# Linear attention's quotient written as a mean less a small term, with a new table of ranks

## The chip, the core and the metric

The kernel runs on one core of a Trainium2 chip. A core has a matrix engine (TensorE, PE in the profile; its weight loads are listed apart as PEld), a vector engine (DVE), a scalar engine for activations (ACT), a general engine (POOL) and a queue that starts transfers (SP). The metric is the device time of one execution in microseconds, the median of several runs.

## The reference, cut to what matters

The whole is two transformer layers on x of 8 x 512 x 128: linear attention, an fp4 feed-forward, causal softmax attention, and a mixture of experts, each behind a layer norm and added to x. The change lies in the first of these:

```python
q = jnp.einsum('bsi,ihd->bshd', x, wq) + bq
k = jnp.einsum('bsi,ihd->bshd', x, wk) + bk
v = jnp.einsum('bsi,ihd->bshd', x, wv) + bv
Q = _feature_map(q)          # elu(t) + 1
K = _feature_map(k)
KV = jnp.einsum('bshd,bshd->bhd', K, v, precision=HI)
Ksum = jnp.sum(K, axis=1)
Z = 1.0 / (Q * Ksum[:, None, :, :] + EPS)       # EPS = 1e-06
attn = Q * KV[:, None, :, :] * Z
out = jnp.einsum('bshd,hdo->bso', attn, wo) + bo
return jax.nn.gelu(out)
```

There are 8 batches (b), 512 positions (s), 16 heads of 64 (h, d): 1024 features. For one feature and one batch, KV and Ksum are single numbers, and the quotient is Q·KV / (Q·Ksum + EPS), position by position.

## The kernel before

The kernel does not issue instructions directly. Its calls are recorded as steps (class `Plan`), each with a rank, and `Plan.ordered` then puts them into one order for all engines, with a model of each step's length: whenever an engine is free, it takes the ready step of the lowest rank whose buffers are to be had. All recorded instructions are issued from one line, 407, so the profile tells them apart by the names of their tiles. `HURRY` and `EMPTY` lower the rank of a dense matmul after an idle stretch, and of the step that reads a PSUM buffer last. `kept_warm` puts matmuls on zeros (tile `mid<-zeros,ident`) into gaps of TensorE's order. Steps on `nc.either` may go to DVE or POOL.

The work of one batch is cut into stages, or lanes: loads, norm, linear, out, fp4, attention, routing, experts. Each call of a stage takes the next entry of the table `TURNS`; `Span` gives the stage's steps ranks that rise along it. In the program the linear attention and fp4 stages of batch b come with the softmax attention, routing and experts of batch b - 1; the ranks decide how they are mixed. PSUM has two double buffers (`pair`), one for the attention outputs (`mid`) and three single ones (`ahead`); a half of a `pair` may be lent to `ahead`.

Linear attention works with features on the 128 partitions and positions along the row, in 8 tiles (c) of 128 features for each batch. For a tile, `elu` multiplies xnT by the weights, and makes elu (less one or not) of it with two ACT steps and one DVE step. `features(c)` does it for k, whose sum over positions comes out of the same DVE step (ks), sums the product with v (kv), does q, and prepares:

- `qf`, q's feature plus one (ACT, `qf<-qf,one_sb`), and `z` = qf·ks + 1e-6 (ACT, `z<-qf,eps_sb,s`);
- `kb` = ks·bv + kv on DVE in one-column steps (`s<-s` and `s<-s,bqkv_sb,s`), and `wk_o`, the output weights with their rows scaled by kb (ACT).

`products(c)` joins two tiles so that one reciprocal does for both: r = z0·z1, q0·z1 and q1·z0 (three products, `r<-z,z` and `qf<-qf,z`), then 1/r on DVE in two halves, then two products with r (`qf<-qf,r`). All of these products stand on POOL. `linear_out` sums the eight matmuls of `wk_o` with these tiles in two groups of four, adds bo, and goes on with the gelu.

On sizes: xnT has two buffers, qf seven, z three, wk_o five; the one-column sums come from twelve buffers `s1`.

Of the kernel before, what the change touches and what calls it, by code (L numbers as in the profile page):

```python
# [9 lines left out]
F32 = mybir.dt.float32  # L10
# [3 lines left out]
AF = mybir.ActivationFunctionType  # L14
ALU = mybir.AluOpType
AX = mybir.AxisListType

P = 128
# [20 lines left out]
class View:  # L39


    def __init__(self, buf, shape, path=()):
        self.buf, self.shape, self.path = buf, tuple(shape), path
# [91 lines left out]
class Plan:  # L135
# [45 lines left out]
    def one_go(self):  # L181
        return OneGo(self)
# [1 line left out]
    def together(self):  # L184
        return Together(self)

    def span(self, lane, low, high):
        return Span(self, lane, low, high)

    def add(self, engine, method, a, k):  # L190
        step = self.open
# [57 lines left out]
    def ordered(self):  # L249
# [12 lines left out]
            for b in s.uses:  # L262
                users[b] = len(b.users)
        ready_at = {s: 0.0 for s in self.steps}
        empties = set()
        for s in self.steps:
            for b in s.uses:
                if b.tag in self.psum and s.engine != "tensor" and (False or max(b.users, key=lambda u: u.number) is s):
                    empties.add(s)
        waiting = {e: [] for e in self.engines}  # L270
        for s in self.steps:
            if not left[s]:
# [11 lines left out]
        while done < len(self.steps):  # L284
            for e in self.HOP:
                while busy[e] <= now:
# [3 lines left out]
                    ahead = HURRY if e == "tensor" and clock.idle(now) else 0.0  # L290
                    for s in sorted(
                        ready,
                        key=lambda s: (s.rank - (ahead if s.work > 0.6 * s.cost else 0.0) - (EMPTY if s in empties else 0.0), s.number),
                    ):
                        if s.port and port > now:
                            continue
                        asked = {}
                        for b in s.takes:
                            asked.setdefault(b.tag, []).append(b)
                        if not all(  # L300
                            all(b in turns[s.lane, t][-len(bs) :] for b in bs)
                            for t, bs in asked.items()
                        ):
                            continue
                        if all(
                            (t not in kept or stuck) and free.has(t, len(bs)) for t, bs in asked.items()
                        ):
                            best = s
                            break

                        kept.update(asked)
# [197 lines left out]
class Span:  # L509


    def __init__(self, plan, lane, low, high):
        self.plan, self.lane, self.low, self.high = plan, lane, low, high

    def __enter__(self):
        self.plan.lane = self.lane
# [2 lines left out]
    def __exit__(self, *_):  # L519
        steps = self.plan.steps[self.first :]  # L520
        total, done = sum(s.cost for s in steps) or 1.0, 0.0
        for s in steps:
            s.rank = self.low + (self.high - self.low) * done / total
            done += s.cost


# [86 lines left out]
def cost(engine, method, out, ins, a, k):  # L613
# [32 lines left out]
    if engine == "gpsimd":  # L646
# [17 lines left out]
    *((f"s4 {lane}", [P, NT], 10, F32) for lane in LANES),  # L664
    ("s1", [P, 1], 12, F32),
    ("xn", [P, NT, D], 1, F32),
    ("xnT", [P, S], 2, F32),
    ("kf", [P, S], 2, F32),
    ("qf", [P, S], 7, F32),
    ("z", [P, S], 3, F32),  # L670
    ("r", [P, S], 1, F32),
    ("y", [P, S], 2, F32),
    ("wk_o", [P, D], 5, F32),
    ("xf", [P, NT, D], 2, F32),
    ("xfT", [P, S], 1, F32),
    ("sc", [P, 44], 4, F32),
# [26 lines left out]

TURNS = {
    "loads": (
        (-3.318, -1.909), (-0.316, -0.059), (0.897, 0.897), (1.614, 1.925),
        (2.836, 3.009), (4.433, 4.682), (4.978, 4.978),
    ),  # L710
    "norm": (
        (-2.124, -2.124), (-0.875, -0.875), (0.083, 0.200), (1.422, 1.904),
        (2.231, 2.231), (3.002, 3.606), (3.880, 4.108), (5.162, 5.409),
    ),
    "linear": (
        (-1.500, -0.940), (-0.500, 0.050), (0.419, 0.790), (2.088, 2.088),
        (2.612, 3.162), (3.422, 3.979), (4.158, 4.730), (4.805, 5.222),
    ),
    "out": (
        (-1.176, -0.826), (-0.386, -0.123), (0.618, 0.709), (1.508, 1.508),  # L720
        (2.508, 3.214), (3.335, 3.734), (4.601, 4.985), (5.739, 6.093),
    ),
    "fp4": (
        (-1.986, -1.736), (-0.900, -0.500), (0.154, 0.510), (1.010, 1.218),
        (2.103, 2.516), (3.487, 3.887), (3.993, 4.270), (5.177, 5.177),
        (5.602, 6.278),
    ),
    "attention": (
        (-0.500, 0.000), (0.000, 0.909), (0.934, 1.761), (2.198, 3.044),
        (3.241, 3.877), (3.954, 4.849), (5.114, 5.848), (6.017, 7.017),  # L730
        (7.193, 8.226),
    ),
    "routing": (
        (1.913, 2.213), (2.979, 3.308), (4.000, 4.223), (5.196, 5.230),
        (6.538, 6.538), (7.103, 7.746), (8.148, 8.148), (8.956, 9.346),
    ),
    "experts": (
        (2.400, 2.713), (3.217, 3.986), (4.222, 5.211), (5.438, 6.138),
        (6.531, 6.863), (7.391, 8.138), (8.571, 9.439), (9.499, 10.378),
    ),  # L740
}

# [2 lines left out]
def block_kernel(  # L745
# [138 lines left out]
    neghalf = const.tile([P, NT], F32, name="neghalf", tag="neghalf")  # L884
    dev.gpsimd.memset(neghalf, -0.5)

    rank = const.tile([P, NT, E], F32, name="rank", tag="rank")
    for e in range(E):
        dev.gpsimd.memset(rank[:, :, e : e + 1], float(E - e))
    eps_sb = const.tile([P, 1], F32, name="eps_sb", tag="eps_sb")  # L890
    dev.gpsimd.memset(eps_sb, 1e-6)
    one_sb = const.tile([P, 1], F32, name="one_sb", tag="one_sb")
    dev.gpsimd.memset(one_sb, 1.0)

    vas = [const.tile([P, NT, H1, VW], F32, name=f"va{i}", tag=f"va{i}") for i in range(2)]
    for t in vas:
# [81 lines left out]
    def linear_attention(b):  # L978

        xnT = normed.pop(b)  # L980

        def elu(c, i, w, tag, **accum):

            pw = new("ahead", [P, S])
            nc.tensor.matmul(pw, w[c // 2][:, ts(c % 2, P)], xnT, start=True, stop=True)
            f = new(tag, [P, S])
            bias = bqkv_sb[:, i, c : c + 1]
            nc.scalar.activation(f, pw, AF.Relu, bias=bias)
            nc.scalar.activation(pw, pw, AF.Exp, bias=bias)
            nc.vector.scalar_tensor_tensor(f, pw, -1.0, f, ALU.add, ALU.min, **accum)  # L990
            return f

        def features(c):

            ks, kv, kb = (new("s1", [P, 1]) for _ in range(3))
            kf = elu(c, 1, wqkv[1], "kf", accum_out=ks)
            nc.vector.tensor_scalar(ks, ks, float(S), None, ALU.add)
            pw = new("ahead", [P, S])
            nc.tensor.matmul(
                pw, wqkv[2][c // 2][:, ts(c % 2, P)], xnT, start=True, stop=True  # L1000
            )
            nc.vector.scalar_tensor_tensor(pw, kf, 1.0, pw, ALU.add, ALU.mult, accum_out=kv)

            nc.vector.tensor_scalar(
                kb, ks, bqkv_sb[:, 2, c : c + 1], kv, ALU.mult, ALU.add
            )
            qf = elu(c, 0, wqkv[0], "qf")
            nc.scalar.activation(qf, qf, AF.Identity, bias=one_sb)
            z = new("z", [P, S])
            nc.scalar.activation(z, qf, AF.Identity, bias=eps_sb, scale=ks)  # L1010
            wk_o = new("wk_o", [P, D])
            nc.scalar.activation(wk_o, wo_sb[c // 2][:, c % 2, :], AF.Copy, scale=kb)
            return qf, z, wk_o

        def products(c):


            (q0, z0, w0), (q1, z1, w1) = features(c), features(c + 1)
            r = new("r", [P, S])
            nc.either.tensor_tensor(r, z0, z1, ALU.mult)  # L1020
            nc.either.tensor_tensor(q0, q0, z1, ALU.mult)
            nc.either.tensor_tensor(q1, q1, z0, ALU.mult)
            for part in (slice(0, 256), slice(256, S)):
                nc.vector.reciprocal(r[:, part], r[:, part])
            nc.either.tensor_tensor(q0, q0, r, ALU.mult)
            nc.either.tensor_tensor(q1, q1, r, ALU.mult)
            return [(w0, q0), (w1, q1)]

        return [p for c in range(0, NC0, 2) for p in products(c)]

    def linear_out(b, pairs):
        y = new("y", [P, S])
        for half in range(2):
            po = new("ahead", [P, S])
            with together():
                for i, (wk_o, qz) in enumerate(pairs[4 * half : 4 * half + 4]):
                    nc.tensor.matmul(po, wk_o, qz, start=(i == 0), stop=(i == 3))
            if half == 0:
                nc.scalar.activation(y, po, AF.Identity, bias=bo_sb)
            else:  # L1040
                nc.vector.tensor_tensor(y, po, y, ALU.add)

        g = new("y", [P, S])
        nc.scalar.activation(g, y, AF.Square)
# [447 lines left out]
    def stage(lane, what, *args):  # L1492
        with plan.span(lane, *next(turns[lane])):
            return what(*args)

    for b in range(NB):
        if b > 1:
            xs[b] = stage("loads", load_x, b)
        normed[b] = stage("norm", normed_T, xs[b], "ahead", "xn", "xnT")
        pairs = stage("linear", linear_attention, b)  # L1500
        stage("out", linear_out, b, pairs)
        if b == 0:
            stage("fp4", fp4_weights)
        stage("fp4", fp4_feed_forward, b)
# [77 lines left out]
```

## Time and profile before

| | us |
|---|---|
| median of three runs | 1132.38 (1130.52 to 1133.14) |
| the profiled execution | 1131.95 |
| its span, first to last instruction | 1130.1 |
| first exponential of the softmax attention starts | 198 |
| last attention output normalised | 1054 |

The profiled execution is 1.85 us longer than its span; all times in the profile count from the span's start. Busy shares are means over the span. The granted clock of TensorE was 0.982 of full speed on average; it was below 1.0 in most slices of the first 226 us. A float32 matmul of 128x128 weights shows up as two records. A row of groups gives the line, the engine, the operation, the tiles written and read, the sizes and count; behind the bar, the busy time, the mean of one in ns, and the engine's idle time just before it with what ended most of it.

### The profile page before, as it was taken

The page shows a single profiled execution, that of the slowest core. Times are in us where ns is not written, and L with a number is a line of the kernel's source. Part 1 is how long each engine was busy: PE and PEld are TensorE (multiplying, and loading weights), DVE is VectorE, ACT ScalarE, POOL GpSimd, SP SyncE. Part 2 cuts the span into 40 slices and gives each one's busy share as a digit, 9 for nine tenths or more (in the row PEclk, how much of TensorE's full clock was granted, in tenths as well). Part 3 has the DMA queues.
Part 4 walks back from the last instruction along what each step waited for, and adds up shares of the span by engine and source line. Part 5 has one row for each costly group of instructions (what it writes and reads, how often), then busy time and mean ns, then how long its engine had stood idle before and what let it go on. Part 6 is the DMA issues. An engine that isn't in the chain of part 4 may idle for free.

```text
span 1130.1 us, 15043 instructions
## 1 busy us (share of the span) xinstructions
PE 1040.2 (92%) x5025; PEld 488.0 (43%) x5025; DVE 830.3 (73%) x1868; ACT 630.8 (56%) x1084; POOL 624.3 (55%) x669
## 2 busy tenths in 40 slices
PE   6667788998899999999998999999999999999998
PEld 2223333344344444444543444454454445445454
DVE  6868879897888967758788968788667765556543
ACT  5756787678786644644578555764443443344311
POOL 6647846676676466237635755467644533441534
PEclk9879989999999999999999999999999999999999
DMA  8000030001101020111012000210002102001000
GB/s 235 1 1 0 1 111 1 21 20 56 39 20 30 10 94 20 58 72 35 26 39 94 19 21 20 95 30 19 20 7 98 39 20 104 21 20 30 1 10 9
DMA packets 30572, 44.31 MB, mean 39 GB/s; under 512 B 4192, under 2 KB 18464, under 8 KB 30496
## 3 DMA queue, kind: packets, MB, share of 16 engines
q1 hardware_dynamic: 30496, 43.37, 11.9%
q8 instruction: 39, 0.64, 0.2%
q14 instruction: 37, 0.30, 0.1%
HBM read 23.95 MB, written 18.87 MB: 38 GB/s over the span
## 4 chain that ended last, share of the span: by engine, by line
PE 57%; DVE 15%; ACT 6%; issue 2%; POOL 1%; DMA 0%; POOLq 0%; DVEq 0%; ACTq 0%
PE ahead L407 31%; PE pair L407 19%; PE mid L407 7%; ACT pr L407 2%; DVE r L407 2%; DVE mx L407 2%; DVE h L407 1%; DVE sc L407 1%; ACT qf L407 1%; DVE s4 routing L407 1%; DVE qf L407 1%; DVE act L407 1%; ACT z L407 1%; DVE kf L407 1%; DVE oh L407 1%
## 5 line engine op out<-in xcount | busy, mean ns | idle before, releaser
L407 ACT ACTIVATE pr<-pair 128x1024 f32<-128x1024 f32 (+1 forms) x192 | 166.7, 879 | 149.2 <-PE pair L407 129.1
L407 DVE TENSOR_REDUCE mx<-pair 128x4 f32<-128x512 f32 (+2 forms) x192 | 198.5, 1041 | 68.4 <-PE pair L407 57.7
L407 POOL TENSOR_SCALAR_AFFINE_SELECT pr<-pr 128x256 f32<-128x256 f32 (+1 forms) x192 | 92.8, 485 | 176.4 <-ACT pr L407 175.6
L407 PE MATMUL pair<-qkT 32*128 32x128 f32 (+7 forms) x1024 | 172.3, 387 | 9.4 <-ACT pr L407 2.7
L407 PEld LDWEIGHTS pair<-qkT 32*128 32x128 f32 (+1 forms) x1024 | 84.4, 183 | 181.8 <-ACT pr L407 52.0
L407 POOL TENSOR_TENSOR act<-act,tw 128x512 f32<-128x512 f32 x64 | 81.3, 1272 | 88.8 <-DVE act L407 80.6
L407 PE MATMUL ahead<-um,b_sb 128*128 128x512 f32 x240 | 122.2, 607 | 0.0
L407 DVE RECIPROCAL r<-r 128x256 f32<-128x256 f32 x64 | 110.3, 1736 | 14.9 <-POOL r L407 14.8
L407 DVE SCALAR_TENSOR_TENSOR act<-act,ahead 128x512 f32<-128x512 f32 x120 | 81.9, 684 | 51.4 <-ACT act L407 38.0
L407 POOL TENSOR_TENSOR qa<-qa,qa 128x704 f32<-128x704 f32 (+4 forms) x60 | 81.2, 1354 | 35.1 <-DVE qa L407 26.2
L407 POOL TENSOR_TENSOR qf<-qf,r 128x512 f32<-128x512 f32 x64 | 80.5, 1278 | 34.5 <-DVE r L407 27.8
L407 PE MATMUL mid<-pr,va 128*10 128x512 f32 (+3 forms) x1024 | 93.3, 435 | 0.0
L407 POOL TENSOR_TENSOR qf<-qf,z 128x512 f32<-128x512 f32 x64 | 80.3, 1270 | 0.0
L407 ACT ACTIVATE act<-ahead 128x512 f32<-128x512 f32 x60 | 35.8, 597 | 72.0 <-PE ahead L407 71.9
L407 PE MATMUL ahead<-act,a_sb 128*128 128x512 f32 x128 | 65.2, 619 | 0.0
L407 POOL TENSOR_TENSOR r<-z,z 128x512 f32<-128x512 f32 x32 | 40.9, 1278 | 41.6 <-ACT z L407 39.3
L407 PE MATMUL ahead<-tT,w_sb 128*128 128x512 f32 x120 | 63.3, 609 | 0.0
L407 ACT ACTIVATE ahead<-ahead,bqkv_sb 128x512 f32<-128x512 f32 x96 | 63.0, 656 | 0.0
L407 PE MATMUL pair<-mask_q,ident 128*128 128x128 bf16 (+1 forms) x384 | 61.6, 242 | 0.0
L407 PE MATMUL ahead<-xnT,wk 128*128 128x512 f32 x100 | 56.7, 650 | 4.8 <-DVE kf L407 2.1
L407 PEld LDWEIGHTS ahead<-um,b_sb 128*128 128x128 f32 x240 | 40.7, 190 | 36.1 <-issue 29.6
L407 ACT ACTIVATE z<-qf,eps_sb,s 128x512 f32<-128x512 f32 x64 | 51.9, 811 | 6.8 <-DVE s L407 5.1
(227 smaller groups left out, 1986.4 us busy)
## 6 DMA issues: line engine op xcount, KB each, us to landing
stacks<-qk SPq DMA_DIRECT2D x32, 512.0 KB
qkT<-stacks SPq DMA_DIRECT2D x128, 128.0 KB
x<-in SPq DMA_DIRECT2D x8, 256.0 KB
qkT<-mr SPq DMA_DIRECT2D x128, 4.0 KB
out<-x SPq DMA_DIRECT2D x8, 256.0 KB
w_sb<-in SPq DMA_DIRECT2D x3, 256.0 KB
wq<-in SPq DMA_DIRECT2D x4, 128.0 KB
wk<-in SPq DMA_DIRECT2D x4, 128.0 KB
```

The costliest lines, as they stand in the source:

```text
L407: getattr(e, method)(*a, **k)
```

## The change

The quotient is rewritten. With m = KV/Ksum and e = 1e-6/Ksum it is Q·KV / (Q·Ksum + 1e-6) = m - m·e / (Q + e). The first part does not depend on the position, so it is taken through the output weights as one column for each batch; only the second part is made position by position.

For two tiles, `z` is now qf + 1 + e, made in place by two ACT steps (the second takes e as its bias in place of a scale and a bias); r = z0·z1 and its reciprocal stay, and each z is multiplied by r once, which leaves 1/z of the other tile. The two products of qf with z are gone, and so are the tiles z. ks, kv, e (`ek`), m (`mean`) and m·e (`part`) are kept as columns of tiles `heads` with 8 columns, and worked on for two tiles at once: three DVE steps of 128x2 (add and max, reciprocal, times 1e-6) and three POOL products or sums of 128x2. `wk_o` is scaled by `part`. In `linear_out` the two groups of matmuls are subtracted, and eight matmuls of one column (wo against `mean`) sum the constant, to which bo is added on DVE; it is then added to y by one more ACT step.

Buffers: xnT 2 to 1, qf 7 to 10, wk_o 5 to 8, z 3 to none, heads 15. Every entry of the table `TURNS` has three ranks in place of two (start, middle, end of the stage's cost, straight between), and all its numbers differ. The rule for `EMPTY` is written in another way for the same steps, and two constant columns are filled in another order, one of them left out.

```diff
@@ class Span
-    def __init__(self, plan, lane, low, high):
-        self.plan, self.lane, self.low, self.high = plan, lane, low, high
+    def __init__(self, plan, lane, low, middle, high):
+        self.plan, self.lane = plan, lane
+        self.low, self.middle, self.high = low, middle, high
...
-            s.rank = self.low + (self.high - self.low) * done / total
+            x = done / total
+            s.rank = (
+                self.low + (self.middle - self.low) * 2 * x if x < 0.5
+                else self.middle + (self.high - self.middle) * (2 * x - 1)
+            )
@@ SBUF
-    ("xnT", [P, S], 2, F32),
+    ("xnT", [P, S], 1, F32),
-    ("qf", [P, S], 7, F32),
-    ("z", [P, S], 3, F32),
+    ("qf", [P, S], 10, F32),
+    ("heads", [P, NC0], 15, F32),
-    ("wk_o", [P, D], 5, F32),
+    ("wk_o", [P, D], 8, F32),
@@ TURNS, two stages of eight
     "linear": (
-        (-1.500, -0.940), (-0.500, 0.050), (0.419, 0.790), (2.088, 2.088),
-        (2.612, 3.162), (3.422, 3.979), (4.158, 4.730), (4.805, 5.222),
+        (-1.423, -1.179, -1.178), (-0.864, -0.431, -0.338), (-0.243, 0.603, 0.672),
+        (1.666, 1.695, 1.695), (2.343, 2.840, 2.840), (3.435, 3.528, 3.798),
+        (4.154, 4.163, 4.728), (4.743, 5.014, 5.199),
     ),
     "experts": (
-        (2.400, 2.713), (3.217, 3.986), (4.222, 5.211), (5.438, 6.138),
-        (6.531, 6.863), (7.391, 8.138), (8.571, 9.439), (9.499, 10.378),
+        (2.273, 2.469, 2.469), (3.172, 3.602, 3.876), (4.261, 4.716, 5.211),
+        (5.506, 5.813, 6.292), (6.478, 6.708, 6.876), (7.030, 7.030, 7.769),
+        (8.494, 8.955, 9.092), (9.670, 10.064, 10.715),
     ),
@@ linear_attention
+        ks, kv, ek, mean, part = (new("heads", [P, NC0]) for _ in range(5))
...
         def features(c):
-            ks, kv, kb = (new("s1", [P, 1]) for _ in range(3))
-            kf = elu(c, 1, wqkv[1], "kf", accum_out=ks)
-            nc.vector.tensor_scalar(ks, ks, float(S), None, ALU.add)
+            kf = elu(c, 1, wqkv[1], "kf", accum_out=ks[:, c : c + 1])
...
-            nc.vector.tensor_scalar(
-                kb, ks, bqkv_sb[:, 2, c : c + 1], kv, ALU.mult, ALU.add
-            )
-            qf = elu(c, 0, wqkv[0], "qf")
-            nc.scalar.activation(qf, qf, AF.Identity, bias=one_sb)
-            z = new("z", [P, S])
-            nc.scalar.activation(z, qf, AF.Identity, bias=eps_sb, scale=ks)
-            wk_o = new("wk_o", [P, D])
-            nc.scalar.activation(wk_o, wo_sb[c // 2][:, c % 2, :], AF.Copy, scale=kb)
-            return qf, z, wk_o
+            return elu(c, 0, wqkv[0], "qf")
 
         def products(c):
-            (q0, z0, w0), (q1, z1, w1) = features(c), features(c + 1)
+            z = [features(c + i) for i in range(2)]
+            two = slice(c, c + 2)
+            nc.vector.tensor_scalar(ks[:, two], ks[:, two], float(S), 1e-15, ALU.add, ALU.max)
+            nc.vector.reciprocal(ks[:, two], ks[:, two])
+            nc.vector.tensor_scalar(ek[:, two], ks[:, two], 1e-6, None, ALU.mult)
+            for i in range(2):
+                nc.scalar.activation(z[i], z[i], AF.Identity, bias=one_sb)
+                nc.scalar.activation(z[i], z[i], AF.Identity, bias=ek[:, c + i : c + i + 1])
+            nc.gpsimd.tensor_tensor(mean[:, two], kv[:, two], ks[:, two], ALU.mult)
+            nc.gpsimd.tensor_tensor(
+                mean[:, two], mean[:, two], bqkv_sb[:, 2, two], ALU.add
+            )
+            nc.gpsimd.tensor_tensor(part[:, two], mean[:, two], ek[:, two], ALU.mult)
             r = new("r", [P, S])
-            nc.either.tensor_tensor(r, z0, z1, ALU.mult)
-            nc.either.tensor_tensor(q0, q0, z1, ALU.mult)
-            nc.either.tensor_tensor(q1, q1, z0, ALU.mult)
-            for part in (slice(0, 256), slice(256, S)):
-                nc.vector.reciprocal(r[:, part], r[:, part])
-            nc.either.tensor_tensor(q0, q0, r, ALU.mult)
-            nc.either.tensor_tensor(q1, q1, r, ALU.mult)
-            return [(w0, q0), (w1, q1)]
+            nc.either.tensor_tensor(r, z[0], z[1], ALU.mult)
+            for some in (slice(0, 256), slice(256, S)):
+                nc.vector.reciprocal(r[:, some], r[:, some])
+            out = []
+            for i in range(2):
+                nc.either.tensor_tensor(z[i], z[i], r, ALU.mult)
+                wk_o = new("wk_o", [P, D])
+                nc.scalar.activation(
+                    wk_o, wo_sb[c // 2][:, i, :], AF.Copy, scale=part[:, c + i : c + i + 1]
+                )
+                out.append((wk_o, z[1 - i]))
+            return out
@@ linear_out
             if half == 0:
-                nc.scalar.activation(y, po, AF.Identity, bias=bo_sb)
+                nc.scalar.activation(y, po, AF.Copy, scale=-1.0)
             else:
-                nc.vector.tensor_tensor(y, po, y, ALU.add)
+                nc.vector.tensor_tensor(y, y, po, ALU.subtract)
+        pc = new("ahead", [P, 1])
+        with one_go():
+            for c in range(NC0):
+                nc.tensor.matmul(
+                    pc, wo_sb[c // 2][:, c % 2, :], mean[:, c : c + 1],
+                    start=(c == 0), stop=(c == NC0 - 1),
+                )
+        same = new("s1", [P, 1])
+        nc.vector.tensor_tensor(same, pc, bo_sb, ALU.add)
+        nc.scalar.activation(y, y, AF.Identity, bias=same)
```

## The prediction

> **What bounds the kernel now.** I read the page first: busy shares, then the chain that ended last.
>
> ```profile
> PE 1040.2 (92%) x5025; PEld 488.0 (43%) x5025; DVE 830.3 (73%) x1868; ACT 630.8 (56%) x1084; POOL 624.3 (55%) x669
> PE 57%; DVE 15%; ACT 6%; issue 2%; POOL 1%; DMA 0%; POOLq 0%; DVEq 0%; ACTq 0%
> ```
>
> TensorE is busy for 92% of the span and carries most of the chain; POOL carries 1% of it. So removing POOL work pays only where POOL makes DVE or TensorE late. An average hides the stages, so the next view is the table of stretches, cut where the first softmax exponential starts (198 us) and where the last attention output is normalised (1054 us). Columns: length, then PE, PEld, DVE, ACT, POOL busy, then clock and DMA.
>
> ```profile
> 0.00:198.00 198.00, 148.29 (x392) 64.00 (x392) 153.35 (x392) 137.28 (x246) 123.70 (x144) 0.92 0.17 50
> 198.00:1054.00 856.00, 822.49 (x4393) 387.93 (x4391) 640.14 (x1401) 480.70 (x814) 468.35 (x500) 1.00 0.12 40
> 1054.00:1130.00 76.00, 69.47 (x244) 36.05 (x242) 36.84 (x77) 12.79 (x24) 32.21 (x26) 0.98 0.02 7
> ```
>
> The start leaves TensorE 50 us idle; DVE is the fullest engine there (77%). In the middle TensorE has only 856 - 822 = 33.5 us of gaps. The tail is 76 us with 6.5 us of gaps. Linear attention, the part that is edited, runs from the beginning to about 780 us.
>
> Of the rows by form, those that the edit touches, and the nearest rows for what it adds:
>
> ```profile
> L407 DVE RECIPROCAL r<-r 128x256 f32<-128x256 f32 x64 | 110.3, 1736 | 14.9 <-POOL r L407 14.8
> L407 POOL TENSOR_TENSOR qf<-qf,z 128x512 f32<-128x512 f32 x64 | 80.3, 1270 | 0.0
> L407 ACT ACTIVATE z<-qf,eps_sb,s 128x512 f32<-128x512 f32 x64 | 51.9, 811 | 6.8 <-DVE s L407 5.1
> L407 ACT ACTIVATE qf<-qf,one_sb 128x512 f32<-128x512 f32 x64 | 46.2, 722 | 11.6 <-DVE qf L407 11.5
> L407 POOL TENSOR_TENSOR qa<-qa,qa 128x256 f32<-128x256 f32 x4 | 2.9, 726 | 2.2 <-DVE qa L407 1.2 <-DVE s L407 0.8
> ```
>
> and from the views of single tiles (min/median/max ns) and the timeline of PE:
>
> ```profile
> L407 DVE TENSOR_SCALAR s<-s x64: 95/146/155, 17.4 to 753.4; 128x1 f32<-128x1 f32 x64
> L407 DVE TENSOR_SCALAR s<-s,bqkv_sb,s x64: 174/273/275, 17.6 to 753.6; 128x1 f32<-128x1 f32 x64
> L407 DVE TENSOR_SCALAR s4 fp<-mv fp x8: 170/170/1261, 75.6 to 843.4; 128x4 f32<-128x4 f32 x8
> 1069.88 1.06 PE L407 MATMUL ahead<-gw_sb,tT 128*128 128x8 f32 x8
> ```
>
> **The change, part by part.** Counts come from the two programs' instruction orders, durations from the rows above.
>
> *POOL.* The 64 products qf·z go: 64 x 1.270 = -81 us. The product for r and the 64 products with r stay, all on POOL in both orders. Added are 96 products of two columns. No row has one. From 128x256 at 726 ns and 128x512 at 1270 the slope is 2.1 ns a column, so about 0.19 us remain at two columns: +18 us. Bounds: the 128x4 memset, 104 ns (10 us in all), and the 128x4 power, 1.01 us (97 us). Net -63 us, off the chain but for its 1%. If they cost a power's 1 us, POOL would gain nothing.
>
> *DVE.* 64 x 0.273 + 64 x 0.146 = -26.8 us. Added: 64 two-column scalar operations at about 0.146 (+9.3), 32 two-column reciprocals at the 128x4 reciprocal's 0.178 (+5.7), 8 one-column additions out of PSUM (+1.5 at 0.19): net -10 us. Bound from the other side: the s4 fp row, four columns, takes 170 ns, but up to 1261, as long as one POOL product; the one-column rows never exceed 155 and 275. If a two-column operation waits like a four-column one, then POOL is in a product about half of the time, a hit waits for half of 1.27 us, and 64 x 0.5 x 0.64 = +20 us turns the net into +10. I take the middle, nothing gained on DVE. This wait lies between the sums ks and z: both tiles' ACT steps stand behind it, and POOL's r behind those; before, z of the first tile waited for its own sum only.
>
> The Trainium skill, "Advanced Engine Details and Errata", section "VectorE Performance Modes", says that the second Vector port is shared with GpSimd and that two-port Vector operations and GpSimd block each other; an even two-column operation within SBUF would be such a one, and by that rule the sum would be the +10. That speaks against the edit, which turns one-column operations into two-column ones; the s4 fp row agrees, but no run here shows a two-column one.
>
> *ACT.* z loses its scale: 64 x (0.811 - 0.722) = -5.7 us; y gets another pass, 8 x 0.68 = +5.5. Nothing.
>
> *TensorE.* 64 one-column matmuls are added (wo against the mean). The nearest row is gw against tT: the same 128x128 f32 weights, eight columns, 8 records in 1.06 us; with the last record's 0.26 us taken off, 0.8/7 = 0.11 us apart, and two records make one matmul: 64 x 0.22 = +14.3 us. If only the columns counted it would be near 0; if they cost the 0.86 us of a full 512-column matmul, 55 us. The weights are loaded alike, so I take the row. They stand in eight groups, three ahead of the first attention product (5 us, in the start's idle time) and five behind it (+9 us on a full engine). The warming matmuls (zeros) go from 44 to 42 and from 16,832 to 14,080 columns: at 0.43 us per record of 512 columns (48 records in 20.79 us in the chain) 2752 x 2 x 0.43/512 = -4.6 us, 3 of it in the middle.
>
> The Trainium skill, "TensorE: Matmul & The Clock Gate", section "Back-to-back issue gap", gives small matmuls a floor of about 60 cycles, 25 ns; by that 128 records would be an estimated 3 us. The row, over four times as long, has weights loaded for every record, so the row decides.
>
> *The table, and the pools.* I sum the dense matmul time in each program's PE order. Up to the first attention product: 120 us before, 130 after. From there to the last normalisation: 769 and 784. Behind it: 62 and 51. DVE ahead of the first copy of the maxima: +5 us, ACT ahead of the first exponential: +3, POOL -18. One xnT buffer in place of two makes the next norm's copy wait for the last matmul on the old one; in both orders every norm's transposes stand behind that matmul already, with other matmuls around them, so I cost it at nothing (if nothing covered it: a 0.58 us copy and as much again in hops for seven batches, 8 us). DMAs are the same in number and order.
>
> **The sum.**
> - Start: DVE is fullest and has 5 us more before attention, ACT 3, POOL 18 less. Bounds -8 (POOL's waits there, the 7.7 us that DVE r stood for POOL r) to +10 (all of the added PE work). I take +4.
> - Middle: +15 of matmuls, -3 of warming: +12. Against it stands what the relief closes of the 33.5 us of gaps; bounds 0 and 33. In this stage 20 us of weight loads wait for POOL's select of pr, and 27 for kf, qf, s, wk_o and their PSUM tiles. I take 14, under half, since DVE gains nothing: -2.
> - Tail: 11 us of matmuls fewer behind the last normalisation, mostly the second to last batch's experts; bounds 0 (routing's own chain is the limit already) and -11. TensorE is 91% busy there, so I take -8.
>
> Sum 4 - 2 - 8 = -6 on the span of 1130.1: 1124. The profiled execution is 1.85 us longer than its span (1131.95), the median of the runs 0.43 more: 1124.1 + 2.3 = **1126 us**, 0.5% faster.
>
> **Rivals.** Changes under 0.2%, 2.3 us, can't be told from none.
> 1. *Slower: TensorE has no room.* The added and moved matmuls are paid in full, because its gaps in the middle are waits on ACT pr (53 us of weight-load waits) and DVE mx (30), which the edit doesn't touch; the two-column DVE steps feed it. Start +4, middle +12, tail 0: 1132 + 16 = 1148. It decides once gaps closed and tail saved are together under 14 us. For it: 92%, and POOL's 1% of the chain. Against: DVE r, qf, kf, z are on the chain too.
> 2. *No change:* the same with the tail's 8 us saved and 8 us of gaps closed: 1132.
> 3. *A large gain:* DVE and TensorE really stood behind POOL. The start gives 8, the middle closes 20 of 33, net -8, the tail 10: 1106. For it: 47 us of waits named above; against: the reciprocals, 110 us of DVE, all stay.
> That the edit doesn't do what it says is excluded for POOL by the order; for the quotient there is still one reciprocal pair for two tiles, as before.
>
> **How the numbers follow.** Forecast 0.38, slower 0.35, no change 0.13, large gain 0.14. Faster by over 0.2%: 0.38 + 0.14 = 0.52; within: 0.13; slower: 0.35. The range goes from the large gain's 1106 to the slow rival's 1148; what lies outside, gains with the whole bound of start and middle or a start at +10 beside a full middle, is under 0.2. The forecast's own range is 1117 to 1130.
>
> **What would show it.** POOL's row qf<-qf,z gone and POOL's busy time near 560 us; the one-column matmuls 0.11 us a record; the two-column DVE rows at 146 ns median, with a maximum over 1 us if they wait for POOL. The first exponential at 198 to 208 us; middle gaps near 20 us; the last normalisation to the end in 66 to 70 us. It is wrong if the gaps stay at 33 us or grow, or if the tail stays at 76 because routing's chain sets it.

## The result, and the profile after

| | median, us | runs from .. to | ratio to before, 95% interval |
|---|---|---|---|
| before | 1132.1 | 1130.5 .. 1133.1 | |
| changed | 1147.8 | 1141.8 .. 1154.8 | 1.0141 [1.0108, 1.0174] |

The change makes the kernel 1.4% slower; 0.5% faster was forecast. The four runs also lie 13 us apart, in place of 2.6. The profiled execution of the changed kernel took 1154.8 us, with a span of 1153.1. Its busy shares and its chain:

```profile
PE 1070.3 (93%) x5149; PEld 508.7 (44%) x5149; DVE 841.5 (73%) x1844; ACT 629.8 (55%) x1092; POOL 563.2 (49%) x700
PE 64%; DVE 22%; ACT 7%; POOL 3%; issue 3%; POOLq 0%; DVEq 0%; ACTq 0%
```

POOL is down to 563 us, as worked out, but TensorE and DVE are both busier than before. The table of stretches, cut at the same two events as before (first exponential, last attention output); the number after POOL is the granted clock:

```profile
0.00:199.00 199.00, 155.14 (x440) 68.26 (x441) 163.57 (x397) 138.81 (x257) 104.48 (x160) 0.96 0.17 50
199.00:1087.00 888.00, 855.06 (x4495) 406.21 (x4493) 648.93 (x1381) 480.29 (x817) 431.82 (x519) 0.97 0.12 38
1087.00:1153.10 66.10, 60.10 (x217) 34.23 (x216) 28.96 (x68) 10.73 (x20) 26.90 (x22) 0.92 0.03 8
```

The start is as long as before (199 against 198 us), the tail 10 us shorter, the middle 32 us longer. In the middle TensorE's gaps are 888 - 855 = 33 us, what they were before: nothing was closed. And the clock there is 0.97 where it was 1.00.

The rows of what was added, from the rows by form (busy, mean ns, idle before) and from the view of the tile `heads` (min/median/max ns):

```profile
L410 DVE TENSOR_SCALAR heads<-heads 128x2 f32<-128x2 f32 x64 | 26.4, 413 | 1.0
L410 PE MATMUL ahead<-heads,wo 128*128 128x1 f32 x128 | 15.8, 253 | 0.0
L410 POOL TENSOR_TENSOR heads<-heads,heads 128x2 f32<-128x2 f32 x64 | 12.7, 199 | 17.5 <-DVE heads L410 14.9 <-POOL heads L410 0.2
```

```profile
L410 DVE TENSOR_SCALAR heads<-heads x64: 104/169/1243, 19.7 to 771.4; 128x2 f32<-128x2 f32 x64
```

The two-column DVE step has a median of 169 ns, but a mean of 413: 23 of the 64 take over 0.3 us, 20 us together, and each of these 23 ends within 0.03 us after a POOL instruction does. The timeline shows one of them beside POOL (start, length, idle before):

```profile
58.40 0.17 DVE L410 RECIPROCAL heads<-heads 128x2 f32<-128x2 f32 x1
58.49 2.48 POOL L410 TENSOR_TENSOR qf<-qf,r 128x512 f32<-128x512 f32 x2 [10.68 <-DVE heads L410]
58.60 1.17 DVE L410 TENSOR_SCALAR heads<-heads 128x2 f32<-128x2 f32 x1
59.87 1.33 ACT L410 ACTIVATE qf<-qf,heads 128x512 f32<-128x512 f32 x2 [2.98 <-DVE heads L410]
```

POOL begins a product at 58.49 and the second product follows 1.24 us later; the DVE step that starts in the first one ends as that ends, at 59.77, and ACT's two steps stand behind it.

The clock comes next. Where it falls, it falls from full to half, for 3.4 us or a multiple of that. Here are three windows of 3.4 us ahead of a fall, each with the half-clock stretch behind it, from the same kind of table:

```profile
200.70:204.10 3.40, 3.40 (x25) 2.29 (x23) 3.40 (x6) 1.83 (x2) 3.40 (x5) 1.00 0.02 5
204.10:214.40 10.30, 10.30 (x43) 4.30 (x43) 5.91 (x11) 2.98 (x5) 4.57 (x9) 0.50 0.00 1
357.70:361.10 3.40, 3.40 (x23) 2.40 (x22) 3.30 (x8) 2.82 (x4) 0.41 (x1) 1.00 0.00 0
361.10:368.00 6.90, 6.90 (x27) 2.72 (x26) 5.30 (x13) 2.16 (x3) 0.81 (x2) 0.51 0.01 2
828.80:832.20 3.40, 3.40 (x31) 2.36 (x29) 1.79 (x4) 1.24 (x2) 1.91 (x2) 1.00 0.00 0
832.20:839.00 6.80, 6.80 (x19) 2.38 (x21) 3.47 (x6) 1.44 (x4) 1.87 (x2) 0.50 0.24 77
```

TensorE is busy without a gap in each window ahead of the fall, and the clock still falls to half for two or three windows. What these windows have in common shows in the timeline of PE ahead of the first fall:

```profile
202.34 0.44 PE L410 MATMUL pair<-qkT 34*128 34x384 f32 x2
202.71 2.33 PE L410 MATMUL ahead<-heads,wo 128*128 128x1 f32 x16
204.97 1.90 PE L410 MATMUL mid<-pr,va 128*10 128x512 f32 x8
```

It is a group of the new one-column matmuls: 16 records that start over 1.6 us or more, in which the array is handed one column for each load of 128x128 weights. The middle of this profile has three more falls, at 296, 481 and 760 us, with no such group ahead; there TensorE was idle for 0.6 to 2.0 us of the window. They make up as much half-clock time, 24 us, as the three shown, so the groups can account for about half of what the middle lost.

Over the four runs, time goes with the clock: spans of 1140.1, 1143.9, 1148.2 and 1153.1 us go with mean clocks of 0.982, 0.977, 0.970 and 0.967. That is 20.5, 26, 34 and 38 us of clock lost ((1 - clock) x span), about 0.75 us of time for each. The kernel before, at a clock of 0.982, lost 20.5 us too, yet took 1130.1: the clock can't be the whole loss.

So there are three suspects: the clock (A), the matmuls' own time (B) and the DVE waits (C). A fourth is the table, which can't be seen in a profile.

### The profile page after: what moved, and what is told of

Read it like the earlier page. It is cut to its first block, busy times and chain, and to the rows that moved or that the text cites. A ratio compares the mean times of both kernels' runs of the same rounds, so it can differ in the third digit from the quotient of the medians.

```text
span 1153.1 us, 15297 instructions
## 1 busy us (share of the span) xinstructions
PE 1070.3 (93%) x5149; PEld 508.7 (44%) x5149; DVE 841.5 (73%) x1844; ACT 629.8 (55%) x1092; POOL 563.2 (49%) x700
## 4 chain that ended last, share of the span: by engine, by line
PE 64%; DVE 22%; ACT 7%; POOL 3%; issue 3%; POOLq 0%; DVEq 0%; ACTq 0%
PE ahead L410 33%; PE pair L410 23%; PE mid L410 8%; DVE r L410 5%; DVE mx L410 2%; ACT qf L410 2%; DVE qf L410 2%; DVE h L410 1%; DVE heads L410 1%; DVE kf L410 1%; DVE ahead L410 1%; DVE sc L410 1%; ACT pr L410 1%; DVE qa L410 1%; ACT kf L410 1%
## 5 line engine op out<-in xcount | busy, mean ns | idle before, releaser
L410 PE MATMUL pair<-qkT 32*128 32x128 f32 (+7 forms) x1024 | 178.7, 395 | 8.2 <-DVE mx L410 3.6
L410 PE MATMUL ahead<-um,b_sb 128*128 128x512 f32 x220 | 114.3, 614 | 0.0
L410 POOL TENSOR_TENSOR qf<-qf,r 128x512 f32<-128x512 f32 x64 | 80.3, 1268 | 62.6 <-DVE r L410 27.3
L410 DVE SCALAR_TENSOR_TENSOR act<-act,ahead 128x512 f32<-128x512 f32 x110 | 75.1, 684 | 48.7 <-ACT act L410 33.9
L410 PE MATMUL mid<-pr,va 128*10 128x512 f32 (+3 forms) x1024 | 97.4, 452 | 0.8 <-POOL pr L410 0.8
L410 ACT ACTIVATE act<-ahead 128x512 f32<-128x512 f32 x54 | 32.1, 595 | 76.0 <-PE ahead L410 76.0
L410 PE MATMUL pair<-mask_q,ident 128*128 128x128 bf16 (+1 forms) x384 | 62.6, 246 | 0.0
L410 PE MATMUL ahead<-xnT,wv 128*128 128x512 f32 x110 | 59.6, 624 | 2.8 <-DVE qf L410 1.4
L410 PE MATMUL ahead<-act,a_sb 128*128 128x512 f32 x112 | 56.9, 617 | 0.0
L410 POOL TENSOR_TENSOR r<-qf,qf 128x512 f32<-128x512 f32 x32 | 40.8, 1275 | 28.5 <-ACT qf L410 28.2
L410 ACT ACTIVATE qf<-qf,one_sb 128x512 f32<-128x512 f32 x64 | 46.2, 722 | 13.4 <-DVE qf L410 13.4
L410 ACT ACTIVATE qf<-qf,heads 128x512 f32<-128x512 f32 x64 | 44.5, 717 | 16.1 <-DVE heads L410 15.0
```

Of the source, the lines that this page charges most:

```text
L410: getattr(e, method)(*a, **k)
```

## The experiments

The planner would put everything in another order if a step changed, and another order can move the time by 1 to 3% by itself (see the runs on the tables below). So in most runs the recorded steps and their order stay, and only the calls that a step issues are exchanged.

**Spread columns.** After the group of eight is recorded:

```diff
+        step = plan.steps[-1]
+        wide = View(pc.buf, (P, S))[:, 0:P]
+        step.calls = [
+            (m, (wide, a[1], a[2].to_broadcast([P, P])), k) for m, a, k in step.calls
+        ]
```

> The changed kernel in its own order; each of the 64 one-column matmuls has its column repeated over 128 columns, and the first column of the result is used. Theory A (clock): the one-column matmuls keep TensorE's sequencer busy while the array streams next to nothing, so the clock is halved just behind them (in the profile of the changed kernel at 204, 361 and 832 us); 128 columns take the same 0.11 us a record, so the clock should stay whole there, mean granted clock 0.98 in place of 0.967 to 0.982, and the median falls to 1140 to 1143 us, with less spread than the 13 us of the changed kernel. Theory B (matmul time alone): nothing changes, 1146 to 1150. Theory C (two-column DVE waits): nothing changes either.

Measured: 1136.7 us (1133.1 to 1140.1), ratio 1.0053 [1.0033, 1.0074]; the changed kernel beside it 1148.9. In the profile (span 1132.0) the groups take about as long as before, 112 ns from record to record against 106, and the clock stays whole where it fell before. Here are the window with the group that stood ahead of the first fall, and the stretch behind it:

```profile
198.40:201.81 3.41, 3.41 (x24) 2.31 (x23) 3.41 (x6) 1.83 (x2) 3.41 (x5) 1.00 0.02 5
201.81:212.05 10.24, 10.21 (x77) 5.40 (x77) 9.03 (x17) 5.62 (x10) 5.97 (x11) 1.00 0.07 20
```

77 records start in the 10.2 us behind the group, in place of 43. The profiled execution is one of the faster ones, with a clock of 0.991; the median run has 0.986, 16 us lost, where the changed kernel's has 0.974, 30 us lost. At 0.75 us each these 14 us are worth 10 of the 12 us gained. A was right, and its gain larger than the 6 to 9 us expected (1140 to 1143 against 1148.9).

**One matmul of eight.**

```diff
+        step = plan.steps[-1]
+        m, a, k = step.calls[0]
+        step.calls = [(m, a, {"start": True, "stop": True})]
```

> The changed kernel in its own order; of each group of eight one-column matmuls only the first is issued, so seven eighths of the constant term are left out of the output. Theory B: 56 matmuls of 0.22 us, 12.3 us, leave TensorE's queue, some 4 us of it in the start's idle time: with theory A's clock on top 1130 to 1134 us, with B alone 1138 to 1141. Theory C or a poorer table as the cause: 1144 to 1148.

Measured: 1131.8 us (1128.5 to 1142.3), 1.0013 [0.9986, 1.0039], as A and B together have it. Taking the matmuls away gives 5 us more by the medians than spreading them, though the two intervals still touch. The middle is 871 us long, as with spread columns (873).

**Single columns on DVE.** For both two-column scalar steps:

```diff
-            nc.vector.tensor_scalar(ks[:, two], ks[:, two], float(S), 1e-15, ALU.add, ALU.max)
+            def by_column(out, src, *rest):
+                nc.vector.tensor_scalar(out[:, two], src[:, two], *rest)
+                plan.steps[-1].calls = [
+                    ("tensor_scalar", (out[:, i : i + 1], src[:, i : i + 1], *rest), {})
+                    for i in range(c, c + 2)
+                ]
+            by_column(ks, ks, float(S), 1e-15, ALU.add, ALU.max)
             nc.vector.reciprocal(ks[:, two], ks[:, two])
-            nc.vector.tensor_scalar(ek[:, two], ks[:, two], 1e-6, None, ALU.mult)
+            by_column(ek, ks, 1e-6, None, ALU.mult)
```

> The changed kernel in its own order; each of the 64 two-column scalar operations on DVE is issued as two of one column, which in the kernel before never waited for POOL. Theory C: the waits of up to 1.24 us behind a POOL product vanish, every one-column row stays under 0.3 us, and the time falls by 5 us or more, to 1143 or less. Theories A and B: within 2 us of the changed kernel, 1146 to 1150.

Measured: 1138.6 us (1137.0 to 1139.5), 1.0066 [1.0042, 1.0091]. Twice as many steps, and no waits (view of the tile `heads`):

```profile
L410 DVE TENSOR_SCALAR heads<-heads x128: 93/144/155, 19.5 to 759.3; 128x1 f32<-128x1 f32 x128
```

128 x 0.144 = 18.4 us of DVE in place of 26.4, and 10 us off the time. The first exponential starts at 190.4 us in place of 199: 9 us are gained in the start, where DVE is the fullest engine. The middle is no shorter (883 us). At the same clock of 0.977 the runs take 1138.4 to 1139.5 us here and 1145.0 to 1145.7 in the changed kernel, so about 7 of the 10 us do not come from the clock. C was right too, though I had held A for the whole.

**The changed kernel again.**

> The changed kernel again, on the same chip as the three above, to compare with. All theories: 1142 to 1155 us; theory A also that the time of each run goes with its granted clock, about 0.75 us for each us of clock lost.

Measured: 1148.9 us (1145.0 to 1154.0), 1.0156 [1.0123, 1.0190]. In its profile (span 1144.0, clock 0.977) the start is 199.3 us, the middle 882, the tail 62.6. Half clocks begin at 204.7, 361.7 and 825.9 us again and at 689.4, each within 2.4 us of the start of the last record of a group of one-column matmuls (204.7, 361.0, 824.4, 687.1). Two other stretches in the middle, at 269.5 and 754.2 us, have no such group. Four of the middle's six groups have a fall beside them here, three in the first profile, and the first profile's longest stretch, 17 us from 481, is missing here: which falls happen differs from run to run.

**Both edits.**

> The changed kernel in its own order with both edits: the one-column matmuls spread over 128 columns (first run: 1136.7 us) and the two-column DVE steps issued by single columns (third run: 1138.6), against 1148.9 for the changed kernel beside them. Theory: two separate costs, the halved clock behind the one-column matmuls and DVE's waits for POOL; then the gains add, 12 + 10 us, and the time is 1125 to 1129, under the kernel before at 1132. If both edits cure the same thing (the clock, or one chain), the time stays at 1134 to 1138.

Measured: 1124.3 us (1121.1 to 1126.4), 0.9932 [0.9915, 0.9949]: 0.7% under the kernel before, and faster than both. The two gains add (24.6 us against 12.2 + 10.3, with the runs on two chips). Its stages:

```profile
0.00:189.40 189.40, 149.78 (x440) 66.21 (x441) 157.10 (x423) 138.57 (x257) 104.55 (x160) 0.98 0.18 52
189.40:1059.60 870.20, 838.20 (x4495) 400.51 (x4493) 644.59 (x1419) 479.76 (x817) 431.87 (x519) 0.99 0.12 39
1059.60:1122.30 62.70, 55.72 (x217) 30.67 (x216) 28.50 (x68) 10.77 (x20) 26.61 (x22) 0.99 0.03 9
```

Against before: start -9, middle +14, tail -13. The middle's gaps are 32 us still.

**Both, with one matmul of eight.**

> As the run above, but of each group of eight one-column matmuls only the first is issued: seven eighths of the constant term are left out. This leaves of the change what it takes away and the table. If TensorE's time in these matmuls costs what the first call showed (1136.7 to 1131.8, 5 us of the 12 that leave), 1120 to 1124 us; if it costs nothing once DVE doesn't wait, the same as the run above.

Measured: 1127.4 us (1119.2 to 1133.8), 0.9961 [0.9937, 0.9985]. That is above the 1120 to 1124 us of the first alternative, and 3 us above the run before it, from which it can't be told apart by the intervals. But the runs again go with the clock, from 1119.2 us at 0.989 to 1133.8 at 0.973. The median run has 0.981, 21 us lost, against 0.992 and 9 us with both edits. At nearly the same clock, leaving the matmuls out is 5 to 7 us faster: 1119.2 us at 0.989 against 1124.2 to 1126.4 at 0.990 with both edits alone (the run above and its repeat below). So B has its share too: TensorE's time in these matmuls costs about half of its 12 us, and here the clock takes that back. The second run, with the DVE waits left in, is much the same in this: a median clock of 0.984, 18 us lost.

Its profile (span 1132.1, one of the slower executions) also limits A. The clock falls at 346.9 us, for 10.2 us, behind this window:

```profile
343.53:346.94 3.41, 3.27 (x21) 1.99 (x20) 3.34 (x6) 2.89 (x5) 0.41 (x1) 1.00 0.00 0
346.94:357.18 10.24, 10.24 (x36) 2.88 (x34) 6.89 (x17) 4.39 (x7) 3.67 (x5) 0.50 0.00 0
```

```profile
343.58 1.06 PE L410 MATMUL ahead<-gw_sb,tT 128*128 128x8 f32 x8
344.50 1.10 PE L410 MATMUL ahead<-qf,wk_o 128*128 128x512 f32 x2
345.53 0.51 PE L410 MATMUL pair<-qkT 34*128 34x512 f32 x2
345.97 0.38 PE L410 MATMUL ahead<-heads,wo 128*128 128x1 f32 x2
346.49 0.50 PE L410 MATMUL pair<-qkT 32*128 32x256 f32 x4
```

TensorE is busy for 3.27 of 3.41 us, with one one-column matmul in place of eight. Four of the routing's eight-column matmuls and the attention's scores, whose weights fill 32 or 34 of 128 rows, take most of the rest; only one matmul is of full size. So a fall doesn't need eight one-column matmuls in a row. That any window with little for the array to do will bring it is a guess from these windows; no run separates it.

**The tables.** First the kernel before with the new table and `Span`, all else as it was:

> The kernel before with the changed kernel's table of three ranks, its quotient and buffers as before. If the new table is better by itself: 1115 to 1128 us. If it fits only the steps that it was made with: 1132 to 1160. No theory on the quotient is decided by this alone; it bounds what the table may have given or taken.

Measured: 1142.7 us (1142.0 to 1144.2), 1.0097 [1.0081, 1.0113], at a clock of 0.992. Then the new quotient with both edits and the old table:

> The quotient of the change with both edits of the first run of this call, but the old table of two ranks. Together with the two runs of this call that have the new one: if the table carries the gain, 1132 us or more; if the quotient does, 1120 to 1132.

Measured: 1157.6 us (1153.0 to 1165.9), 1.0241 [1.0202, 1.0281]. By that test the table carries the gain; but the run before it shows that the new table brings none to the old steps. Each table is worse by 1 to 3% under the other's steps, and neither is better by itself. So the table alone does not explain the loss, and the quotient can't be judged without a table of its own.

**The routing's thin matmuls, spread too.** The 32 matmuls of eight columns get their columns repeated sixteen times:

```diff
+        gw16 = gw_sb.unsqueeze(1).to_broadcast([P, P // E, E])
+        plan.steps[-1].calls = [
+            (m, (whole[:, ts(t, P)].rearrange("p (k e) -> p k e", e=E), a[1], gw16), k)
+            for t, (m, a, k) in enumerate(plan.steps[-1].calls)
+        ]
```

> The version with both edits (1124.3 us in its first run), and the routing's 32 eight-column matmuls (gw against tT) spread over 128 columns as well, in the same order. Theory A: they are the other matmuls that stream next to nothing, eight batches of 0.9 us; a half clock stands right behind them in the profile of the changed kernel's tail at 1098 us, but in none of the three stretches left in the middle of the version with both edits, so 0 to 3 us less than that version; if any short stretch of thin matmuls triggers the half clock, up to 5 us less.

> The version with both edits again, on the same chip as the run above: 1121 to 1127 us, 0.6 to 0.8% under the kernel before.

Measured: 1124.2 us, 0.9934 [0.9915, 0.9954], against 1125.0, 0.9941 [0.9921, 0.9962]: no difference. Spreading the routing's matmuls gains nothing beside the other two edits. Two readings in the expectation were off: the changed kernel's half clock at 1098.4 us begins ahead of the routing's matmuls (1101.0), not behind them, and the middle of the version with both edits has two half-clock stretches (622.7 and 742.2 us), not three.

## Why the prediction was wrong

By the stages of the sum, with the changed kernel's second profile (span 1144.0), which took 1145.7 us, 2 to 3 us under its medians:

| | forecast | measured | both edits |
|---|---|---|---|
| start | +4 | +1 | -9 |
| middle | -2 | +26 | +14 |
| tail | -8 | -13 | -13 |

- *Middle, the relief.* "I take 14" of the gaps closed is the step that failed first. The gaps stayed at 33 us with POOL 61 us less busy, and at 32 us with the DVE waits cured too: almost nothing of them closed, the sign that the prediction had set for being wrong. The added matmuls then lengthen the stage, +12 by the sum, +14 measured with both edits and a clock of 0.99. The relief was to come in part from the 20 us of weight loads that waited for POOL's select of pr; they still wait 22.5 us. The waits on pr and mx, named under the first rival, stayed as well. Taking 14 us, near half of the gaps, for closable had no row behind it. The weight-load waits in the middle (us in all, how often, the longest), three rows of before and three with both edits:

```profile
PEld pair L407 <- ACT pr L407: 53.1, 91, 1.5
PEld pair L407 <- DVE mx L407: 29.5, 47, 1.2
PEld mid L407 <- POOL pr L407: 20.0, 30, 0.8
PEld pair L410 <- ACT pr L410: 55.4, 89, 1.3
PEld pair L410 <- DVE mx L410: 30.3, 45, 1.4
PEld mid L410 <- POOL pr L410: 22.5, 30, 1.0
```

- *TensorE, the one-column matmuls.* Their time was right (0.106 us a record against 0.11). That they cost time alone was wrong: the sum had no term for the clock. By the run with spread columns some 12 us of the median are this, and with it goes most of the spread (0.75 us for each us of clock lost). Before's profile showed the clock at 0.78 to 0.94 only in slices where TensorE also stood idle, and I read it as a thing of idle stretches.
- *DVE, the two-column steps.* The wait was named, and priced from the s4 fp row: 9 to 30 us, measured 26. But "the middle, nothing gained on DVE" carried no price into the start, where the steps stand between the sums and z and DVE is the fullest engine. They cost 9 to 10 us, by the single-column run. That the start's +4 lies near the measured +1 is luck: without the waits the start is 9 us shorter than before, past the bound of -8, and the waits hid it.
- *The rule on two-port operations* ("Advanced Engine Details and Errata" of the Trainium skill, "VectorE Performance Modes") decided against the edit, and the runs agree: one-column steps never took over 155 ns, two-column ones up to 1243, beside POOL. All 23 long steps end with a POOL instruction, and the single-column run shows the cost of the width; the shared port itself no run shows.
- *POOL* was right: 0.194 us a product, 563 us busy. *ACT* was right. *The small-matmul floor* of the other page was no guide where weights are loaded for every record: 106 ns, not 25.
- *Tail.* The mechanism was right, its size 13 in place of 8, past its bound of 11: TensorE's busy time there fell from 69.5 to 55.7 us.
- *The rivals.* The slow one gave 1148, and the time is there, but in part by luck: its +12 in the middle is in the measurement, its tail of 0 isn't, and the clock, which it did not have, makes up the difference. The large gain did not come; what the change takes away is worth 9 us in the start once the waits are gone.

## What to carry to other kernels

A matmul had two prices here: its time, and what happened to the granted clock around it. Groups of thin matmuls often came with a halved clock though TensorE was busy throughout; repeating their one column to 128, at 112 ns a record in place of 106, took 12 us off. A narrow DVE step beside POOL's long products was best issued one column at a time: twice 0.144 us in place of 0.17 to 1.24. Judge an edit of a planned kernel with the order held fixed: a table that was not made for the steps moved the time by 1 to 3% here, as much as the edits or more.

## What the runs showed of the hardware that was not expected

- The clock can halve behind a window in which PE is 100% busy in the records (3.40 of 3.40 us, then 0.50). The Trainium skill, "TensorE: Matmul & The Clock Gate", section "Part 1: The HAM clock gate", ties the gate to how busy TensorE was in windows of 3.4 us. The stretches here are multiples of that (3.4, 6.8, 10.2 and 17.1 us), but busy in the sense of the profile's records is not enough to keep the clock.
- For f32 weights of 128x128, one column and 128 columns take nearly the same: 106 and 112 ns a record.
- A DVE TENSOR_SCALAR of 128x2 took 0.10 to 1.24 us, the long ones ending with a POOL instruction; one of 128x1 took 0.09 to 0.16 us beside the same POOL work.
